# A four-layer convolution chain on one core: tiles kept as sums and differences of neighbours along the width

## The chip, the cores and the metric

The kernel runs on one core of a Trainium2 chip. A core has TensorE (matrix products, PE in the profile, with its weight loads as PEld), VectorE (DVE), ScalarE (ACT), GpSimd (POOL) and SyncE (SP, which here issues most of the DMA transfers). Data lies in the chip's memory (HBM) and is brought into the on-chip buffer (SBUF) by DMA; TensorE writes its products to PSUM, from where VectorE and ScalarE take them. The metric is the device time of one execution, in microseconds (us). Before the change it is 2877.34 us, the median of three runs (2877.28 to 2879.65).

## What is computed

The input x has 4 images of 64 channels of 256 x 256 fp32 values. Four layers follow one another.

Layers 0, 1 and 3 are long convolutions. For each channel c the filter is an outer product of one vector along the rows and one along the width, so that the convolution is two one-dimensional ones, each cut to the first 256 outputs, and a residual:

```
k = jnp.einsum('ijk,imk->ijmk', hx, hy)[0]
...
y = jnp.fft.irfft2(u_f * k_f, s=(fft_size, fft_size))[..., :L, :L]
out = y + x * bias[:, None, None]
```

The vectors hx and hy come from a small network of sines. Layer 2 is a Haar transform in both directions, two 64 x 64 channel mixes with a soft threshold on every coefficient, the sum of both, the inverse transform and a residual:

```
f1 = haar2d(x)
for i in range(v.shape[0]):
    f4 = jnp.einsum('bchw,oc->bohw', f1 * v[i], conv_w[i])
    acc = acc + jnp.sign(f4) * jax.nn.relu(jnp.abs(f4) - tau[i])
return haar2d(acc, inverse=True) + x
```

The first level of the Haar transform along the width replaces each pair of neighbours by their sum and their difference.

## The kernel before, in words

Each one-dimensional convolution is a product with a 256 x 256 triangular Toeplitz matrix, of which two blocks of 128 x 256 and 128 x 128 are multiplied. `toeplitz` fetches, by one DMA of 256 KB per layer and channel, a tile of 128 x 2 x 256 in which each partition holds the filter vector one place further on (one half for the rows, one for the width). `contract` issues four matmuls: the image tile is the stationary operand, the Toeplitz tile, read backwards, is the moving one. TensorE handles fp32 in two records for each matmul. A channel takes two `contract`s per layer: `first` (rows, then ScalarE copies the product out of PSUM, line 267) and `second` (width, then VectorE adds the residual, line 284). The tile comes out transposed after each, so that two give the image the right way round.

For each of the four images the stages are:

- `convolutions`: 64 channels through layers 0 and 1. Then `pairs` (lines 329 and 330) forms sums and differences of neighbours with two VectorE operations; these go to HBM (`keep`) and into `levels`, the further Haar levels along the width (two levels on VectorE, the shorter ones on GpSimd, lines 342 and 343). `split`, `rest` and `down` do the transform along the rows on TensorE; the coefficients go to HBM.
- `mixing`: 64 groups of coefficients. TensorE mixes channels (line 441), VectorE and ScalarE scale (460, 465), threshold (469 to 480) and add (486) into the large tile `z`. `N_ACT` says how many sixteenths of the scaling ScalarE takes.
- `inverse`: for each channel the inverse transform. `rows` (533, 534) and, for the first 16 channels, `cols` on TensorE; `join` adds the kept sums and differences (line 555) and unfolds them into neighbours (lines 558 and 559); then layer 3 follows (`last`) and the result leaves by a DMA on ScalarE's queue. For the first three images every third channel is put off: its tile goes to HBM (`late`), and `convolution` takes it through layer 3 during the mixing of the last image, leaving on SP's queue.

All stages are put on one time axis in units of a tick. `PLACE` gives each step its offset in ticks, `events` is sorted by that time, and the steps are issued in that order; the tile framework then puts the instructions of each engine into a queue of its own, worked off strictly in order, with waits between engines. The convolutions of image b + 1 are spread over the mixing of image b and end where its inverse begins. `BUFS` and the pools set how many copies of a tile there are.

The filters are made at the start by `filters`; its `end` writes both vectors of a layer to HBM (`pads`), from where `toeplitz` reads.

Of the kernel before, what the change touches and what calls it, by code (L numbers as in the profile page):

```python
# [9 lines left out]
F32 = mybir.dt.float32  # L10
# [6 lines left out]
B, C, S, EMB, ORD = 4, 64, 256, 33, 64  # L17
P = 128
ROW = S + P

GT = 4
BUFS = {"res": 1, "y": 5, "co": 3}

N_ACT = (12, 12, 12, 8)

PLACE = {
    "load": 0.714,
    "a0": 1.643,
# [6 lines left out]
    "y1 sum": 4.429,  # L35
    "pairs": 4.639,
    "keep": 4.929,
# [26 lines left out]
    "y3 sum": 3.542,  # L64
    "out": 4.537,
    "level": 0.6,
# [4 lines left out]
    "l y3 sum": 2.783,  # L71
    "l out": 4.4,
    "l mix load": -0.977,
# [25 lines left out]
def conv_seq_kernel(ctx, tc, x, fz, fw, bias, decay, haar, haar_row, factors, vt, taut, wmix, out):  # L99
# [44 lines left out]
    scales = dram.tile([S // 4 // GT, P, 2, GT, 16], F32, name="scales")  # L144
    pads = [dram.tile([C, 2, ROW], F32, name=f"pad{layer}") for layer in range(3)]
    late = dram.tile([B, C, P, 2, S], F32, name="late")

# [11 lines left out]
    def filters(layer, queue):  # L159
# [32 lines left out]
        def end():  # L192
            ps = bank(f"fo{layer}").rearrange("p m s -> p (m s)")[:, :S]
            nc.tensor.matmul(ps, fw_sb[:, 2 * P : 3 * P], st["h"], start=True, stop=True)
            f = part(ROW)
            nc.vector.memset(f[:, S:], 0.0)
            nc.vector.scalar_tensor_tensor(f[:, :S], ps, dsb[:, S:], dsb[:, :S], ALU.mult, ALU.mult)
            for axis, queue in enumerate((nc.scalar, nc.sync)):
                queue.dma_start(pads[layer][:, axis, :], f[axis * C : (axis + 1) * C])
            st["f"] = f  # L200
# [40 lines left out]
    def toeplitz(layer, c, name):  # L241

        t = tp.tile([P, 2, S], F32, name=name, tag="toep")
        nc.sync.dma_start(t, ap(pads[layer], c * 2 * ROW, [[1, P], [ROW, 2], [1, S]]))
        return t
# [3 lines left out]

    def contract(ps, src, t):  # L250

        for m in range(2):
            nc.tensor.matmul(ps[:, m, :], src[:, 0, m * P : (m + 1) * P], t[:, ::-1], start=True, stop=False)  # L253
            nc.tensor.matmul(ps[:, m, P:], src[:, 1, m * P : (m + 1) * P], t[:, : P - 1 : -1], start=False, stop=True)  # L254

    def first(b, st, key, layer, new):


        def product(c):
            s = st[c]  # L260
            s["p" + new] = bank(f"p{new}_{b}_{c}")
            contract(s["p" + new], s[key], s[layer][:, 0, :])

        def copy(c):
            s = st[c]
            a = s[new] = io.tile([P, 2, S], F32, name=f"{new}_{b}_{c}", tag="mid")
            nc.scalar.copy(a, s["p" + new])  # L267

        return [product, copy]

    def second(b, st, key, layer, res, new, tag, ahead=None):


        def product(c):
            s = st[c]
            if ahead is not None:
                s[ahead] = toeplitz(ahead, c, f"t{ahead}_{b}_{c}")
            s["p" + new] = bank(f"p{new}_{b}_{c}")
            contract(s["p" + new], s[key], s[layer][:, 1, :])

        def residual(c):
            s = st[c]
            y = io.tile([P, 2, S], F32, name=f"{new}_{b}_{c}", tag=tag, bufs=BUFS[tag])
            nc.vector.scalar_tensor_tensor(y, s[res], bsb[:, layer, c : c + 1], s["p" + new], ALU.mult, ALU.add)  # L284
            s[new] = y

        return [product, residual]
# [26 lines left out]
    def convolutions(b, ticks, in_parts=(), border=None):  # L314
# [7 lines left out]
        def load(c):  # L322
            xt = io.tile([P, 2, S], F32, name=f"x_{b}_{c}", tag="in", bufs=3)
            nc.sync.dma_start(xt, x[b, c].rearrange("(k p) w -> p k w", p=P))
            st[c] = {"x": xt, 0: toeplitz(0, c, f"t0_{b}_{c}")}

        def pairs(c):
            v = st.pop(c)["y1"].rearrange("p k (w e) -> p k w e", e=2)
            nc.vector.tensor_add(sums[:, c % 4], v[:, :, :, 0], v[:, :, :, 1])
            nc.vector.tensor_sub(sd[:, c % 8, 1], v[:, :, :, 0], v[:, :, :, 1])  # L330

# [50 lines left out]
        def away(c):  # L382
# [5 lines left out]
        work = zip(  # L388
            ("load", "a0", "a0 copy", "y0", "y0 sum", "a1", "a1 copy", "y1", "y1 sum", "pairs", "keep"),
            [  # L390
                load,
                *first(b, st, "x", 0, "a0"),
                *second(b, st, "a0", 0, "x", "y0", "y", ahead=1),
                *first(b, st, "y0", 1, "a1"),
                *second(b, st, "a1", 1, "y0", "y1", "res"),
                pairs,
                store,
# [111 lines left out]
    def inverse(b, start, put_off):  # L509
# [42 lines left out]
        def join(c):  # L552
            ps = st[c]["pw"]
            t = io.tile([P, 2, 2, P], F32, name=f"t_{b}_{c}", tag="res", bufs=BUFS["res"])
            nc.vector.scalar_tensor_tensor(t, st[c]["r"], 0.5, ps, ALU.mult, ALU.add)
            u = io.tile([P, 2, S], F32, name=f"u_{b}_{c}", tag="y", bufs=BUFS["y"])
            v = u.rearrange("p m (w e) -> p m w e", e=2)
            nc.vector.tensor_add(v[:, :, :, 0], t[:, 0], t[:, 1])
            nc.vector.tensor_sub(v[:, :, :, 1], t[:, 0], t[:, 1])
            st[c]["u"] = u  # L560
# [20 lines left out]
        for c in range(C):  # L581
            for name, stage in zip(("sooner", "early", "fetch", "rows"), (sooner, early, fetch, rows)):
                at(start + c + PLACE[name], stage, c)
            turn = start + c
            if c < 16:
                at(start + c + PLACE["halves"], halves, c)
                at(start + c + PLACE["cols"], cols, c)
                turn += 1
            at(turn + PLACE["join"], join, c)
            if c in put_off:  # L590
                at(turn + PLACE["aside"], aside, c)
            else:
                shift = (0.0, 0.0)
                if put_off:
                    shift = ((-0.27, -0.342), (0.23, 0.158))[c % 3]
                for name, stage in zip(("a3", "a3 copy", "y3", "y3 sum", "out"), last(b, st)):
                    at(turn + PLACE[name] + shift[name[0] != "a"], stage, c)

    def last(b, st, queue=nc.scalar):
        return [  # L600
            *first(b, st, "u", 2, "a3"),
            *second(b, st, "a3", 2, "u", "y3", "co"),
            lambda c: queue.dma_start(out[b, c].rearrange("(k p) w -> p k w", p=P), st.pop(c)["y3"]),
        ]

    def convolution(which, ticks):

        for (b, c), tick in zip(which, ticks):
            st = {}

            def load(c, b=b, st=st):
                u = io.tile([P, 2, S], F32, name=f"v_{b}_{c}", tag="in", bufs=3)
                nc.sync.dma_start(u, late[b, c])
                st[c] = {"u": u, 2: toeplitz(2, c, f"t2_{b}_{c}")}

            for name, stage in zip(("l load", "l a3", "l a3 copy", "l y3", "l y3 sum", "l out"), [load, *last(b, st, nc.sync)]):
                at(tick + PLACE[name], stage, c)
# [156 lines left out]
```

## Time and profile before

| what | value |
|---|---|
| median of three runs | 2877.34 us |
| the profiled execution, its own time | 2875.0 us |
| its span (first to last instruction) | 2873.2 us |
| TensorE busy | 2819.8 us (98%) |
| VectorE busy | 2498.0 us (87%) |
| ScalarE busy | 2080.4 us (72%) |
| GpSimd busy | 339.4 us (12%) |
| DMA, mean | 226 GB/s |

Busy time is the time in which an engine has an instruction in hand; matmuls are pipelined, one begins before the last has ended, and their ends are modelled, so a short gap between two can stay unseen. In the views below, "L284" is line 284 of the kernel, `y<-x,bsb,py` says which tile is written from which, then shapes and counts; "busy, mean" are total us and mean ns of one; the idle time ahead of the group and what ended it follow.

The stages on the span's axis: the start to about 30 us; convolutions of the first image to about 430 us; mixing of the first image together with the second's convolutions to about 900; its inverse to about 1080; the same for the second image (1080 to 1728) and the third (1728 to 2376); mixing of the last image with the channels put off to about 2660; the last inverse to the end.

### The profile page before, as it was taken

How to read it: one execution, taken by the hardware profiler on the slowest of the kernel's cores; microseconds unless marked ns; L12 is line 12 of the kernel's file. 1: busy time of each engine (PE TensorE's matmuls, PEld its weight loads, DVE VectorE, ACT ScalarE, POOL GpSimd, SP SyncE). 2: the span in 40 equal slices, each digit the busy share in tenths (PEclk: the TensorE clock that was granted, in tenths of full speed). 3: DMA queues.
4: the chain of work that ended last, by engine and by line, in shares of the span. 5: the costliest groups of instructions: out<-in, count | busy, mean ns of one | idle time of the engine just before them, and what ended most of it. 6: DMA issues, size and time to landing. Idle time of an engine off the chain costs nothing. (4 is left out here: it accounts for less than half of the span.)

```text
span 2873.2 us, 52387 instructions
## 1 busy us (share of the span) xinstructions
PE 2819.8 (98%) x16566; PEld 2550.2 (89%) x16566; DVE 2498.0 (87%) x4263; ACT 2080.4 (72%) x4950; POOL 339.4 (12%) x644
## 2 busy tenths in 40 slices
PE   8999999999999999999999999999999999999999
PEld 6899998888888898998898998998888998888998
DVE  4655558999999779999999779999999779999985
ACT  2333338999995558998995658999995659998554
POOL 0111111121121001221221001221121000000000
PEclk9999999999999999999999999999999999999999
DMA  5877777666676986777777986777777988787786
GB/s 162 260 231 231 230 234 223 208 211 205 202 213 214 291 251 197 215 213 214 209 207 235 299 257 195 216 213 213 212 208 233 299 265 235 230 238 213 224 241 200
DMA packets 599367, 649.77 MB, mean 226 GB/s; under 512 B 48465, under 2 KB 517044, under 8 KB 598964
## 3 DMA queue, kind: packets, MB, share of 16 engines
q1 hardware_dynamic: 536996, 578.61, 68.2%
q10 hardware_dynamic: 62096, 67.82, 6.7%
q8 instruction: 134, 2.20, 0.3%
q14 instruction: 141, 1.16, 0.1%
HBM read 426.77 MB, written 219.48 MB: 225 GB/s over the span
## 5 line engine op out<-in xcount | busy, mean ns | idle before, releaser
L253 PE MATMUL py<-t,a 128*128 128x256 f32 x3072 | 922.2, 382 | 9.9 <-ACT a L267 9.2
L267 ACT COPY a<-pa 128x512 f32<-128x512 f32 x768 | 478.9, 624 | 495.5 <-PE pa L254 453.4
L465 ACT ACTIVATE f<-px,vt 128x64 f32<-128x64 f32 x2816 | 610.6, 367 | 101.4 <-DVE f L460 101.0
L254 PEld LDWEIGHTS py<-t,a 128*128 128x128 f32 x3072 | 583.4, 190 | 79.3
L254 PE MATMUL py<-t,a 128*128 128x128 f32 x3072 | 590.0, 274 | 0.0
L253 PEld LDWEIGHTS py<-t,a 128*128 128x128 f32 x3072 | 497.3, 191 | 51.1 <-ACT a L267 19.3
L441 PE MATMUL px<-wb,f 128*128 128x256 f32 x2048 | 487.6, 380 | 7.4 <-ACT f L465 7.3
L441 PEld LDWEIGHTS px<-wb,f 128*128 128x128 f32 x2048 | 369.0, 190 | 49.8 <-ACT f L465 10.2
L343 POOL TENSOR_TENSOR sd<-less 128x128 f32<-128x128 f32 (+4 forms) x320 | 192.7, 602 | 1855.5 <-DVE less L342 1537.6
L526 ACT COPY zc<-z 128x512 f32<-128x512 f32 x256 | 281.9, 1104 | 108.4 <-PE pw L534 99.6
L476 DVE TENSOR_TENSOR mag<-mag,vt 128x1024 f32<-128x1024 f32 x256 | 316.6, 1237 | 12.2 <-ACT mag L469 11.3
L480 DVE SCALAR_TENSOR_TENSOR mag<-mag,f 128x1024 f32<-128x1024 f32 x256 | 316.5, 1238 | 0.0
L253 PE MATMUL pa<-t,y 128*128 128x256 f32 x1024 | 308.9, 383 | 6.7 <-DVE y L284 5.2
L253 PE MATMUL pa<-t,x 128*128 128x256 f32 x1024 | 305.7, 380 | 0.0
L469 ACT ACTIVATE mag<-f 128x1024 f32<-128x1024 f32 x256 | 295.7, 1155 | 2.7 <-DVE z L486 0.4
L366 DVE TENSOR_TENSOR sp<-sd,sp 128x512 fp32r<-128x512 f32 x256 | 179.8, 702 | 127.8 <-ACT sp L361 126.7
L472 ACT ACTIVATE f<-f 128x1024 f32<-128x1024 f32 x256 | 285.8, 1116 | 3.5
L253 PE MATMUL pa<-t,u 128*128 128x256 f32 x772 | 232.1, 382 | 6.5 <-ACT w L540 2.8
L284 DVE SCALAR_TENSOR_TENSOR y<-x,bsb,py 128x512 f32<-128x512 f32 x256 | 190.7, 745 | 42.1 <-PE py L254 41.8
L254 PEld LDWEIGHTS pa<-t,y 128*128 128x128 f32 x1024 | 194.5, 190 | 26.3
L254 PEld LDWEIGHTS pa<-t,x 128*128 128x128 f32 x1024 | 194.6, 190 | 26.3
L284 DVE SCALAR_TENSOR_TENSOR y<-y,bsb,py 128x512 f32<-128x512 f32 x256 | 190.6, 745 | 27.7 <-PE py L254 27.3
(72 smaller groups left out, 4406.6 us busy)
## 6 DMA issues: line engine op xcount, KB each, us to landing
t<-pad SPq DMA_DIRECT2D x768, 256.0 KB, 4.1
x<-in_x SPq DMA_DIRECT2D x256, 256.0 KB, 3.8
coef<-co SPq DMA_DIRECT2D x256, 256.0 KB, 3.2
f<-coef SPq DMA_DIRECT2D x256, 256.0 KB, 3.1
r<-keep SPq DMA_DIRECT2D x256, 256.0 KB, 4.1
out_y<-y ACTq DMA_DIRECT2D x193, 256.0 KB, 4.2
keep<-sums SPq DMA_DIRECT2D x256, 128.0 KB, 2.9
keep<-sd SPq DMA_DIRECT2D x256, 128.0 KB, 2.8
```

The costliest lines, as they stand in the source:

```text
L253: nc.tensor.matmul(ps[:, m, :], src[:, 0, m * P : (m + 1) * P], t[:, ::-1], start=True, stop=False)
L254: nc.tensor.matmul(ps[:, m, P:], src[:, 1, m * P : (m + 1) * P], t[:, : P - 1 : -1], start=False, stop=True)
L267: nc.scalar.copy(a, s["p" + new])
L284: nc.vector.scalar_tensor_tensor(y, s[res], bsb[:, layer, c : c + 1], s["p" + new], ALU.mult, ALU.add)
L343: engine.tensor_tensor(t[:, :, :, half:length], v[..., 0], v[..., 1], ALU.subtract)
L441: nc.tensor.matmul(ps[:, q, h, :], f[:, q, h * P : (h + 1) * P], wb.rearrange("p r n -> p (r n)"), start=True, stop=True,)
L465: nc.scalar.mul(f4[:, j], px[:, j], scale(g, 0)[:, j : j + 1])
L469: nc.scalar.activation(mag, st[g]["f4"], AF.Abs)
L472: nc.scalar.activation(st[g]["f4"], st[g]["f4"], AF.Sign)
L476: nc.vector.tensor_sub(mag, mag, over(g, 1, 16))
L480: nc.vector.scalar_tensor_tensor(mag, mag, 0.0, st[g]["f4"], ALU.max, ALU.mult)
L526: nc.scalar.copy(a.rearrange("p h k i -> p (h k) i"), z[:, c // 16, :, :, c % 16].rearrange("p i x -> p x i"))
```

## The change

Every image tile of layers 0, 1 and 3 is now kept as sums and differences of neighbours along the width, as `[128, 4, 2, 64]`: for each row half and width half, 64 sums and then 64 differences. The rows' convolution does not mind. For the width, the Toeplitz matrix is written in this basis: a block that takes sums (or differences) gives outputs as sums and as differences, and the two outputs lie side by side in memory. TensorE therefore reads the moving operand with a step of two elements, and the product arrives in PSUM as 64 sums, 64 differences and so on, contiguous.

- The host lays x out in rows of the two halves, with even and odd places apart, and puts the output together again; x and the output move as 2 KB per partition.
- `pairs` is now ahead of layer 0: two adds on GpSimd form sums and differences of x (`butterflies`). The two operations of `pairs` behind layer 1 are gone; the residual of layer 1 (line 284 before) is now two operations of 256 values, which write `sums` and `sd` directly.
- `join` loses its unfolding (558, 559) and its single operation of 512 (555) becomes two of 256 that write the tile `u`.
- Behind layer 3 comes a new step `neighbours`: two adds on GpSimd (on VectorE for the very last channel) unfold the result into `out`, which the DMA then takes.
- The filters: the rows' vector goes to `pads` as before, the width's is turned by six VectorE operations on 64 partitions into pairs (`runs`) and written to HBM. `toeplitz` issues two DMAs instead of one, of 128 KB each.
- Tiles x, xb, y0, u, v and out share the buffers `y`, now 9; `res` is gone. x is loaded 1.7 ticks earlier; "out" leaves 0.66 ticks later ("l out" 0.4).

```diff
-    "load": 0.714,
+    "load": -1.0,
+    "pairs": 0.1,
+    "bands": 0.714,
...
-    "pairs": 4.639,
...
-    "out": 4.537,
+    "neighbours": 3.543,
+    "out": 5.2,
...
-    "l out": 4.4,
+    "l neighbours": 3.48,
+    "l out": 4.8,
...
-            for axis, queue in enumerate((nc.scalar, nc.sync)):
-                queue.dma_start(pads[layer][:, axis, :], f[axis * C : (axis + 1) * C])
+            nc.sync.dma_start(pads[layer], f[:C])
+            g0, g1, g2 = (f[C:, i : i + S : 2] for i in range(3))
...
+            nc.vector.tensor_add(sums, g0, g2)
+            nc.vector.tensor_sub(less, g0, g2)
+            nc.vector.scalar_tensor_tensor(w[:, 0, :P, 0], sums, 0.5, g1, ALU.mult, ALU.add)
+            nc.vector.tensor_scalar(w[:, 0, :P, 1], less, -0.5, None, ALU.mult)
+            nc.vector.tensor_scalar(w[:, 1, :P, 0], less, 0.5, None, ALU.mult)
+            nc.vector.scalar_tensor_tensor(w[:, 1, :P, 1], sums, -0.5, g1, ALU.mult, ALU.add)
+            nc.scalar.dma_start(runs[layer], w)
...
-        nc.sync.dma_start(t, ap(pads[layer], c * 2 * ROW, [[1, P], [ROW, 2], [1, S]]))
+        nc.sync.dma_start(t[:, 0], ap(pads[layer], c * ROW, [[1, P], [1, S]]))
+        nc.sync.dma_start(
+            t[:, 1],
+            ap(runs[layer], c * 4 * RUN, [[2 * RUN, 2], [2, H], [1, S]]),
+        )
...
+    def along_width(ps, src, t):
+
+        t = t.rearrange("p (h n e) -> p h e n", e=2, h=2)[:, ::-1, :, ::-1]
+        v = ps.rearrange("p k (h e n) -> p k h e n", h=2, e=2)
+        for k in range(2):
+            for m in range(2):
+                nc.tensor.matmul(
+                    v[:, k, 1] if m else v[:, k],
+                    src[:, m, k * P : (k + 1) * P],
+                    t[:, 0] if m else t,
...
+    def butterflies(engine, t, name):
+
+        new = io.tile([P, 4, 2, H], F32, name=name, tag="y", bufs=BUFS["y"])
+        engine.tensor_add(new[:, :, 0], t[:, :, 0], t[:, :, 1])
+        engine.tensor_sub(new[:, :, 1], t[:, :, 0], t[:, :, 1])
+        return new
...
+            if new == "y1":
+                for e, to in enumerate((sums[:, c % 4], sd[:, c % 8, 1])):
+                    to = to.rearrange("p k (h n) -> p (k h) n", h=2)
+                    nc.vector.scalar_tensor_tensor(to, s[res][:, :, e], scale, ps[:, :, e], ALU.mult, ALU.add)
...
         def pairs(c):
-            v = st.pop(c)["y1"].rearrange("p k (w e) -> p k w e", e=2)
-            nc.vector.tensor_add(sums[:, c % 4], v[:, :, :, 0], v[:, :, :, 1])
-            nc.vector.tensor_sub(sd[:, c % 8, 1], v[:, :, :, 0], v[:, :, :, 1])
+            st[c]["x"] = butterflies(nc.gpsimd, st[c]["x"], f"xb_{b}_{c}")
...
-            nc.vector.scalar_tensor_tensor(t, st[c]["r"], 0.5, ps, ALU.mult, ALU.add)
-            u = io.tile([P, 2, S], F32, name=f"u_{b}_{c}", tag="y", bufs=BUFS["y"])
-            v = u.rearrange("p m (w e) -> p m w e", e=2)
-            nc.vector.tensor_add(v[:, :, :, 0], t[:, 0], t[:, 1])
-            nc.vector.tensor_sub(v[:, :, :, 1], t[:, 0], t[:, 1])
+            u = io.tile([P, 4, 2, H], F32, name=f"u_{b}_{c}", tag="y", bufs=BUFS["y"])
+            r, w = (t.rearrange("p e k (h n) -> p e (k h) n", h=2) for t in (st[c]["r"], ps))
+            for e in range(2):
+                nc.vector.scalar_tensor_tensor(u[:, :, e], r[:, e], 0.5, w[:, e], ALU.mult, ALU.add)
...
+        def neighbours(c):
+            engine = nc.vector if b + 1 == B and c + 1 == C else nc.gpsimd
+            st[c]["y3"] = butterflies(engine, st[c]["y3"], f"out_{b}_{c}")
```

## The prediction

> **What bounds the kernel now.** I read the page's busy line first, then a table of busy time by stage, then the groups of instructions by shape, then the timeline of GpSimd and VectorE in the mixing stage.
>
> ```profile
> PE 2819.8 (98%) x16566; PEld 2550.2 (89%) x16566; DVE 2498.0 (87%) x4263; ACT 2080.4 (72%) x4950; POOL 339.4 (12%) x644
> ```
>
> TensorE is busy in all but 53.4 of 2873.2 us, at a granted clock of 1.00. An edit that only relieves another engine can win from these pauses alone. By stage (window, its length, then PE, PEld, DVE, ACT, POOL busy):
>
> ```profile
> 432.00:936.00 504.00, 492.23 (x2771) 438.92 (x2770) 488.31 (x818) 435.31 (x1177) 90.49 (x150) 1.00 0.70 210
> 936.00:1080.00 144.00, 141.24 (x930) 130.58 (x930) 107.39 (x212) 83.10 (x121) 0.00 (x0) 1.00 0.87 272
> 1080.00:1512.00 432.00, 429.83 (x2413) 386.99 (x2412) 425.80 (x700) 386.28 (x1085) 89.88 (x140) 1.00 0.71 210
> ...
> 2376.00:2664.00 288.00, 278.39 (x1523) 248.32 (x1522) 285.32 (x413) 268.73 (x686) 0.00 (x0) 1.00 0.77 228
> ```
>
> The reader should see two things. In the mixing stages VectorE is as full as TensorE (488 of 504, 426 of 432). In the last one (2376 to 2664) VectorE, at 285 of 288, is the fuller, and there the change takes nothing from it. The groups that the change touches or that price it:
>
> ```profile
> L253 PE MATMUL py<-t,a 128*128 128x256 f32 x3072 | 922.2, 382 | 9.9 <-ACT a L267 9.2
> L254 PE MATMUL py<-t,a 128*128 128x128 f32 x3072 | 590.0, 274 | 0.0
> L526 ACT COPY zc<-z 128x512 f32<-128x512 f32 x256 | 281.9, 1104 | 108.4 <-PE pw L534 99.6 <-DVE z L486 1.8 <-PE pu L547 1.5
> L284 DVE SCALAR_TENSOR_TENSOR y<-y,bsb,py 128x512 f32<-128x512 f32 x256 | 190.6, 745 | 27.7 <-PE py L254 27.3
> L361 ACT CAST sp<-sd 128x512 fp32r<-128x512 f32 x256 | 180.2, 704 | 8.1 <-POOL sd L343 8.1
> L555 DVE SCALAR_TENSOR_TENSOR t<-r,pw 128x512 f32<-128x512 f32 x192 | 131.7, 686 | 67.5 <-PE pw L534 58.8 <-DMA r<-keep 5.0
> L329 DVE TENSOR_TENSOR sums<-y 128x256 f32<-128x256 f32 x256 | 108.8, 425 | 2.7
> L558 DVE TENSOR_TENSOR u<-t 128x256 f32<-128x256 f32 x256 | 108.8, 425 | 6.3
> L187 DVE SCALAR_TENSOR_TENSOR z<-z 128x256 f32<-128x256 f32 x27 | 11.2, 423 | 0.4
> L197 DVE SCALAR_TENSOR_TENSOR z<-fo,z 128x256 f32<-128x256 f32 x3 | 1.5, 484 | 3.1 <-PE fo L194 3.1
> ```
>
> Last, GpSimd, which gets the new adds. In the convolutions of the first image (72 to 432) a group of its adds, then the timeline in the mixing stage, GpSimd and VectorE:
>
> ```profile
> L342 POOL TENSOR_TENSOR less<-less 128x128 f32<-128x128 f32 x16 | 6.3, 393 | 0.0
> ```
>
> ```profile
> 714.23 3.86 POOL L343 TENSOR_TENSOR sd<-less 128x128 f32<-128x128 f32 x1 [27.66 <-DVE less L342]
> ```
>
> ```profile
> 714.34 1.22 DVE L476 TENSOR_TENSOR mag<-mag,vt 128x1024 f32<-128x1024 f32 x1
> 715.47 2.36 DVE L480 SCALAR_TENSOR_TENSOR mag<-mag,f 128x1024 f32<-128x1024 f32 x2
> 717.74 0.42 DVE L460 TENSOR_TENSOR f<-px,vt 128x256 f32<-128x256 f32 x1
> ```
>
> An add of 128 values takes 0.39 us in one place and 3.86 us in the other, where it stands until VectorE leaves operations with two SBUF operands (476, 480) for one that reads PSUM (460). I take it that GpSimd advances only while VectorE reads PSUM or is idle.
>
> **The change, part by part.** The sum is against the profiled execution, 2875.0 us (span 2873.2 and 1.8 around it); the median of the runs is 2.3 us above that, and the same 2.3 is added at the end. Under 0.2% (5.8 us) is about what a measurement cannot tell from no change.
>
> *TensorE.* Number and size of the matmuls stay, and the order of its queue all but stays. New is the step of two in the moving operand of `py`: 3072 x 256 + 3072 x 128 = 1.18 million columns. No matmul of the trace reads with a step. From below: VectorE reads with a step of two in line 329 (425 ns) and without one in line 187 (423): 0 us; a gain is excluded, since no matmul gets smaller. From above: ScalarE's copy 526 reads 16 elements apart, 1104 ns against 704 for the cast 361, 0.78 ns per element, times 1.18 million: +921 us. I take 0, since 329 has this very step.
> [...]
>
> *VectorE.* Removed: `pairs`, 256 x (425 + 424 ns) = 217 us; the unfolding in `join`, as many operations of the same 425, 217 us. Halved operations: the residual of layer 1, one of 745 becomes two of 484 (line 197 reads PSUM and a scalar in SBUF like these), +57 us; `join`, one of 685 becomes two. For these 512 to 256 values costs 685 - 256 x 1.02 = 424 (the slope from 423 at 256 in line 187 to 685 at 512), so +0.16 x 256 = +42 us. Sum: 2498 - 217 - 217 + 57 + 42 = 2163 us. In the mixing stages a channel loses 0.85 - 0.22 = 0.63 us; a channel takes 288/38 = 7.6 us there (38 residuals per layer between 1224 and 1512), so VectorE falls from 99% to some 91% and TensorE alone is the bound.
>
> What that is worth: TensorE's pauses between 432 and 2376 are 12 + 3 + 2 in the rows above, 2 in 1512 to 1728 and some 5 in the third image, 24 us. A matmul's record runs on 0.16 us past the start of the next (382 ns recorded, 216 apart in the timeline), so each of some sixty pauses hides that much more: 34 us. VectorE ends some of them directly (residual, `w`, `u`) and others by way of ScalarE, which waited 101 us for line 460. I take 60%: -20 us. Bounds: 0, if ScalarE or instruction supply is next in line everywhere, and -34.
>
> *GpSimd.* 1022 adds of 256 values. Price of one with the port free: 393 ns for 128 and 312 for 64 in the same stretch give 1.27 ns a value, so 556; twice 393 is the upper end, 786. I take 600. In mixing, a channel brings 1.2 us, and a quarter of a `levels` burst (ten adds, 0.2 to 0.4 us each where the port is free, 2.7 in all), 0.7: 1.9 us of free port per 7.6. Free is: two residuals' worth of PSUM reads, 0.75 + 0.97, line 460 with 0.42, and 0.6 idle, together some 2.5 us. It fits (75%). The wait added is that of `a0` for `xb`, and GpSimd runs 1.54 ticks ahead (a tick is 288/41 = 7.0 us, so 10.8 us): a burst of `levels` stretched to 2.7/0.33 = 8 us before a pair is about absorbed. I take 0; lower end 0, since nothing can end sooner by it; the upper end is a rival below. In the inverse stages VectorE mostly reads PSUM, so two thirds of a pair in a 3.0 us tick is free.
>
> The last mixing stage: 63 pairs, 76 us of GpSimd beside a full VectorE. The timeline has line 366 at 0.76 us with GpSimd beside it and 0.69 without, so up to 0.07 us on each operation of two SBUF operands. Four in each of 64 groups, half of them touched: +9; part of it lies in pauses, so I take +6. Ends: 0, and +76 if all of GpSimd's time came out of VectorE's. "l out" on SP now waits for GpSimd, and loads of `f`, `v` and Toeplitz tiles queue behind it; 1.32 ticks (4.2 us each) are left for about 4 us.
> [...]
>
> *DMAs.* SP issues 768 more, 0.36 us each in the timeline: 276 us on a queue that issues about 0.9 ms in all. Between loads it waits for buffers anyway: 0. Bytes stay; x and the output go in 2 KB rows, which can only help the 0.87 share of the inverse: 0.
>
> *Ends.* Six operations on 128 values per filter, 0.29 us each: layer 1's filter starts 0.4 us later and the first product with `runs` finds its tile about on time: +0.5 (0 to +3). The last channel adds two operations of 425 before its DMA: +0.8. Buffers `y`: x, xb and y0 take three of nine per channel, so xb waits for the xb three channels back, freed 0.5 tick earlier: 0.
>
> Sum: 2875.0 - 20 + 6 + 1.3 = 2862.3, plus 2.3: **2865 us**. Its own range, with pauses from 0 to -34 and the last mixing from 0 to +15: 2844 to 2872 and a little over.
>
> **Rivals.**
> *GpSimd comes too late* (slower, 0.25). For: the 3.86 us add, and 75% of the port in use. Against: when TensorE waits, VectorE idles and the port comes free. It decides once VectorE leaves less than 1.9/7.6 = 25% of its time; then each of the 192 channels in mixing waits. At 0.3 us each, +58, less 10 us of the gain that remains: 2877 + 48 = 2925; at 0.1 us, 2887.
> *The step costs TensorE time* (slower, 0.10). `py` takes 3072 x (216 + 110 ns) = 1001 us; each 5% of that is +50 us: 2915 and up, to 3786 at the upper end.
> *VectorE's relief is hidden* (0.17): ScalarE and the last mixing stage hold the same pauses, -5 + 6 + 1: 2875 to 2880.
> *All pauses go* (0.05): -34 and most of 10 in the last mixing: 2835 to 2842.
>
> **How the numbers follow.** Forecast 0.43, the rivals as given. Faster by over 0.2% is below 2871.6: 0.40 of the forecast and 0.05: 0.45. Same: 0.17 hidden and 0.02: 0.19. Slower: 0.36 with 0.01 of the forecast. The range, 2842 to 2925, leaves out the last case, the step and a little of the late GpSimd.
>
> **What would show it.** Right: lines 289 and 275 with the same means (382 and 274 ns); VectorE near 2160 us; TensorE's pauses between 432 and 2376 at half; GpSimd near 1.3 to 2 ms busy. Wrong: 289 with a longer mean than 275 (the step), or waits of PE for POOL `xb`, and of SPq for POOL `out` (GpSimd late).

## The result, and the profile after

The changed kernel takes 3578.03 us (median of four runs, 3576.39 to 3580.83) against 2877.31 us: a ratio of 1.2432, interval 1.2417 to 1.2447, so 24% slower or some 700 us. The forecast was 2865 us with a range up to 2925; it was wrong in sign and size. The profiled execution after has a span of 3576.0 us.

The page of the changed kernel, its busy line, then the busy tenths of TensorE and the DMA engines in 40 slices:

```profile
PE 3069.0 (86%) x16566; PEld 2637.8 (74%) x16566; DVE 2345.1 (66%) x3774; ACT 2083.7 (58%) x4950; POOL 1161.9 (32%) x1666
...
PE   6777777999988889988987879989888788999987
...
DMA  4555555565565665666655665565655666666665
```

TensorE was busy in all but 53 us before; now it stands for 507. No compute engine is full over the span, and the DMA engines, busy for 4 to 6 tenths of the time on the mean, move 182 GB/s where they moved 226. So work seems to wait for transfers although the DMA engines as a whole have room. The chain that ended last could be followed back over some 21% of the span; by line, in shares of the whole span, it has one transfer at its head:

```profile
DMA t<-run 5%; POOL out L301 2%; POOL out L300 2%; PE py L289 1%; DMA r<-keep 1%; PE pa L275 1%; DMA out_y<-out 0%; DMA v<-late 0%; PE px L499 0%; DVE mag L534 0%; DVE mag L538 0%; DVE y L340 0%; PE pw L591 0%; DVE z L544 0%; ACT zc L584 0%
```

Pieces of that chain near the end (start, duration, what):

```profile
3405.43 9.39 DMA t<-run
3414.84 8.79 DMA t<-run
3423.64 8.83 DMA t<-run
3432.49 8.61 DMA t<-run
3441.12 8.73 DMA t<-run
```

From 3395 to 3555 us, in the second half of the last inverse, the chain is nothing but 18 loads of the new width half, one behind the other, 7.4 to 10.0 us each and most of them 8.6 to 9.4. Each is 128 KB, and its time runs from issue to landing, so a wait behind a load still in the air is in it. Before, one load of the whole tile, 256 KB, landed in a median of 4.1 us:

```profile
t<-pad SPq DMA_DIRECT2D x768, 256.0 KB, 4.1
```

The timeline of SP's queue in the first convolutions, after (start, duration, line, what):

```profile
229.83 0.51 SPq L261 DMA_DIRECT2D t<-run  x1
230.43 2.22 SPq L390 DMA_DIRECT2D keep<-sums  x1
232.75 0.38 SPq L391 DMA_DIRECT2D keep<-sd  x1
233.22 0.41 SPq L260 DMA_DIRECT2D t<-pad  x1
```

and the same lines in the kernel before:

```profile
218.54 0.33 SPq L333 DMA_DIRECT2D keep<-sums  x1
218.97 0.39 SPq L334 DMA_DIRECT2D keep<-sd  x1
219.45 0.40 SPq L244 DMA_DIRECT2D t<-pad  x1
```

The transfer's own issue is short (0.51 us), but the next one behind it takes 2.22 us instead of 0.33. So the queue from which nearly all loads come stands as well. Waits of TensorE and ScalarE after that hardly existed before (engine, line, what was waited for, us, times, longest):

```profile
PE pa L275 <- DMA t<-pad: 147.2, 155, 4.9
...
ACT a L315 <- DMA t<-run: 66.6, 16, 10.9
...
PE pa L275 <- POOL xb L301: 59.2, 36, 3.9
```

The third line is the forecast's rival, GpSimd too late. It is the smallest of the three, but not the only sign of it: SP waits 100.4 us for `out` (line 665), and `out` has 4% of the span in the chain above.

By stage, from the first and last mixing product of each image (us; convolutions of the first image and the start, then the mixings and inverses of the images):

| kernel | start and conv. | mix 1 | inv. 1 | mix 2 | inv. 2 | mix 3 | inv. 3 | mix 4 | inv. 4 |
|---|---|---|---|---|---|---|---|---|---|
| before | 447 | 399 | 217 | 435 | 213 | 435 | 210 | 271 | 246 |
| after | 637 | 448 | 285 | 500 | 295 | 499 | 293 | 312 | 308 |
| outermost 2 alone, on the kernel before | 641 | 448 | 283 | 504 | 292 | 503 | 288 | 303 | 308 |
| after, run in two halves | 474 | 420 | 227 | 462 | 231 | 462 | 229 | 313 | 255 |
| the same without the butterflies | 470 | 399 | 212 | 441 | 220 | 440 | 215 | 274 | 250 |
| and with a step of one | 469 | 396 | 212 | 435 | 218 | 435 | 213 | 272 | 243 |

Two shapes of loss are in it. After, all stages are longer, most of all those without mixing. With the run in two halves, 117 of some 200 us lie in the mixings, 56 in the inverses and 27 at the start.

### The profile page after: what moved, and what is told of

It is laid out like the page before. It is cut to its first block, busy times and chain, and to the rows that moved or that the text cites. A ratio compares the mean times of both kernels' runs of the same rounds, so it can differ in the third digit from the quotient of the medians.

```text
span 3576.0 us, 54536 instructions
## 1 busy us (share of the span) xinstructions
PE 3069.0 (86%) x16566; PEld 2637.8 (74%) x16566; DVE 2345.1 (66%) x3774; ACT 2083.7 (58%) x4950; POOL 1161.9 (32%) x1666
## 2 busy tenths in 40 slices
DMA packets 535380, 650.20 MB, mean 182 GB/s; under 512 B 50001, under 2 KB 387316, under 8 KB 534964
## 5 line engine op out<-in xcount | busy, mean ns | idle before, releaser
L289 PE MATMUL py<-t,a 128*128 128x256 f32 (+1 forms) x6144 | 1237.9, 345 | 95.4 <-ACT a L315 91.6
L300 POOL TENSOR_TENSOR xb<-x 128x256 f32<-128x256 f32 x256 | 238.2, 930 | 1487.3 <-DMA x<-in_x 1290.5
L300 POOL TENSOR_TENSOR out<-y 128x256 f32<-128x256 f32 x255 | 215.9, 847 | 903.2 <-DVE y L340 855.2
L275 PE MATMUL pa<-t,y 128*128 128x256 f32 (+1 forms) x2048 | 395.8, 337 | 117.9 <-DMA t<-pad 64.7
L275 PE MATMUL pa<-t,xb 128*128 128x256 f32 (+1 forms) x2048 | 392.9, 335 | 116.1 <-POOL xb L301 59.2
L275 PEld LDWEIGHTS pa<-t,xb 128*128 128x128 f32 x2048 | 335.3, 193 | 167.8 <-issue 68.0
L340 DVE SCALAR_TENSOR_TENSOR y<-u,bsb,py 128x512 f32<-128x512 f32 x193 | 144.0, 746 | 373.2 <-issue 335.0
L340 DVE SCALAR_TENSOR_TENSOR y<-xb,bsb,py 128x512 f32<-128x512 f32 x256 | 190.2, 743 | 229.8 <-issue 107.1
L275 PE MATMUL pa<-t,u 128*128 128x256 f32 (+1 forms) x1544 | 300.0, 339 | 39.6 <-DMA t<-pad 27.6
L275 PEld LDWEIGHTS pa<-t,u 128*128 128x128 f32 x1544 | 260.9, 198 | 73.8 <-PE pw L592 33.5
```

The lines of the kernel that those rows point to most:

```text
L275: nc.tensor.matmul(ps[:, m, k * P :], src[:, k, m], t[:, : k * P - 1 if k else None : -1], start=(k == 0), stop=(k == 1),)
L289: nc.tensor.matmul(v[:, k, 1] if m else v[:, k], src[:, m, k * P : (k + 1) * P], t[:, 0] if m else t, start=(m == 0), stop=(m == 1),)
L300: engine.tensor_add(new[:, :, 0], t[:, :, 0], t[:, :, 1])
L340: nc.vector.scalar_tensor_tensor(y, s[res], scale, ps, ALU.mult, ALU.add)
```

## Theories

What differs in the slow transfer is the form of its source: `[[2 * RUN, 2], [2, H], [1, S]]`, two groups of 64 rows. Theory A: the size of the outermost dimension, 2, sets on how many DMA engines the transfer is put. I had not weighed it in the forecast. No view names the engines of a transfer, but the end of the changed kernel speaks for it: SP's last issues are two loads of the width half at 3551.65 and 3552.95 us with one plain load between them, and some 4 us later, when at most these and the rest of two outputs are in the air, the row is (window, length, PE, PEld, DVE, ACT, POOL busy, clock, DMA share of 16 engines, GB/s):

```profile
3557.30:3562.10 4.80, 4.80 (x19) 4.25 (x18) 1.50 (x3) 0.06 (x1) 1.42 (x2) 0.50 0.13 48
```

A share of 0.13 is the time of 2.1 of the 16 engines. The kernel before has 0.54 and 164 GB/s in 2850 to 2854 us, around its last plain loads (issued from 2848.94 us on). For other sizes of the outermost dimension the runs below show the time alone. The rivals: 768 more issues on SP; the pattern's form as such; GpSimd's adds; the step of two. The experiments take them one by one, first on the kernel before, then by undoing parts of the change.

## The experiments

### The pattern alone, and two plain loads, on the kernel before

The kernel before, with the width half fetched by a load of its own from two copies of the vector, the second 64 places on:

```diff
-        nc.sync.dma_start(t, ap(pads[layer], c * 2 * ROW, [[1, P], [ROW, 2], [1, S]]))
+        nc.sync.dma_start(t[:, 0], ap(pads[layer], c * 3 * ROW, [[1, P], [1, S]]))
+        nc.sync.dma_start(t[:, 1], ap(pads[layer], (c * 3 + 1) * ROW, [[ROW, 2], [1, P // 2], [1, S]]))
```

> The kernel before, with one thing added: the width half of each Toeplitz tile is fetched by a DMA of its own whose source has an outermost dimension of two (2 x 64 rows of 1 KB, the second 64 from a shifted copy of the vector), as the changed kernel fetches its pairs. TensorE, VectorE and GpSimd work as before. Theory (the pattern of two confines the transfer to few DMA engines, SP's next issues wait behind it): most of the 700 us, 3200 to 3600. Rival (one more DMA per tile on SP is what costs): as dear as the run with two plain DMAs. Rivals (the step of two costs TensorE, or GpSimd is late): 2870 to 2900, since neither is in this kernel.

Measured: 3569.77 us, 1.2402 (1.2377 to 1.2427). Nothing of the new basis is in this kernel, and it is nearly as slow as the changed one; its stages agree with those after within 10 us each. Pieces of the chain of this kernel near the end (start, duration, what):

```profile
3408.18 8.82 DMA t<-pad
3417.02 8.84 DMA t<-pad
3425.87 8.82 DMA t<-pad
```

The other kernel has two loads as well, each of 128 plain rows:

```diff
-        nc.sync.dma_start(t, ap(pads[layer], c * 2 * ROW, [[1, P], [ROW, 2], [1, S]]))
+        for k in range(2):
+            nc.sync.dma_start(t[:, k], ap(pads[layer], (c * 2 + k) * ROW, [[1, P], [1, S]]))
```

> The kernel before, with each Toeplitz tile fetched by two DMAs of 128 rows instead of one, both with a single step over the 128 partitions: 768 more issues on SP, as in the changed kernel, and nothing else. Theory (confinement): 2877, within 15. Rival (number of issues): 3300 or more.

Measured: 2882.99 us, 1.0017 (1.0007 to 1.0026). The 768 extra issues cost some 4 us. They are not the cause.

### The run in two loads of 64 partitions

The changed kernel, with the outermost dimension of 2 taken out of the pattern and into a loop:

```diff
-        nc.sync.dma_start(
-            t[:, 1],
-            ap(runs[layer], c * 4 * RUN, [[2 * RUN, 2], [2, H], [1, S]]),
-        )
+        for i in range(2):
+            nc.sync.dma_start(t[i * H : (i + 1) * H, 1], ap(runs[layer], (c * 2 + i) * 2 * RUN, [[2, H], [1, S]]))
```

> The changed kernel, with the pattern of two undone: the pairs are fetched by two DMAs of 64 partitions each, 1536 more issues on SP than before. Theory (confinement): nearly all of the 700 us goes; what is left is the step of two on TensorE (first records of 231 and 116 ns against 216 and 110 make 3072 x 21 ns = 65 us) and the forecast of -12: 2930, from 2890 to 2980. Rival (number of issues): above 3578. Rival (GpSimd late): above 3300.

Measured: 3072.84 us, 1.0675 (1.0659 to 1.0691): 505 us are back with the same bytes to the same places. Its transfers (KB each, median us from issue to landing):

```profile
t<-run SPq DMA_DIRECT2D x1536, 64.0 KB, 3.4
```

195 us over the kernel before stay, where the theory expected 2890 to 2980 us in all. They must belong to the rest of the change.

### Outermost 4 and 16

Two loads of 64 changed both the size of the outermost dimension and the pattern's form. So the kernel before once more, with 4 (and then 16) copies of the vector, 32 (8) places apart:

```diff
-    pads = [dram.tile([C, 2, ROW], F32, name=f"pad{layer}") for layer in range(3)]
+    pads = [dram.tile([C, 5, ROW], F32, name=f"pad{layer}") for layer in range(3)]
...
+            for j in range(1, 4):
+                nc.scalar.dma_start(pads[layer][:, j + 1, : ROW - j * (P // 4)], f[C:, j * (P // 4) :])
...
-        nc.sync.dma_start(t, ap(pads[layer], c * 2 * ROW, [[1, P], [ROW, 2], [1, S]]))
+        nc.sync.dma_start(t[:, 0], ap(pads[layer], c * 5 * ROW, [[1, P], [1, S]]))
+        nc.sync.dma_start(t[:, 1], ap(pads[layer], (c * 5 + 1) * ROW, [[ROW, 4], [1, P // 4], [1, S]]))
```

> The kernel before with the width half of the Toeplitz tile fetched by a DMA of its own whose source pattern has an outermost dimension of 4 (four copies of the vector in memory, each 32 places further on, and 32 rows from each); the same data arrives. With an outermost 2 this kernel took 3570 us and the last loads stood 8.8 us apart in the chain; with no outer dimension 2883. Theory A, the outermost dimension sets on how many DMA engines the transfer is put: half the duration, about 4.4 us a load; a channel of the last stage takes about 4 us without the change, so the time falls back to 2885 to 3150. Theory B, any pattern of several rows that isn't one plain run of 128 is slow, whatever its outermost size: 3570 again.

> The same with an outermost dimension of 16 (sixteen copies, each 8 places further on, 8 rows from each). Theory A, by the number of engines: all of the loss is gone, 2878 to 2900, with 45 more writes at the start that may cost a few us. Theory B, by the form of the pattern: 3570 again.

Measured: 2910.28 us with 4, 1.0109 (1.0092 to 1.0126), and 2914.26 with 16, 1.0122 (1.0107 to 1.0137). The form of the pattern is the same as with 2; 660 and 656 of its 692 us are gone. The version with 16 missed its expected range by 14 us: most of what it loses lies at the start, where its 45 extra writes of the vector stand, for the first mixing product comes at 479 us instead of 447, and the stages after it sum to 2434 against 2426. With 4 the start is 13 us longer, and the first three inverses together 22. The loads of the version with 16 (KB each, median us from issue to landing), the same median as in the kernel with two plain loads:

```profile
t<-pad SPq DMA_DIRECT2D x1536, 128.0 KB, 3.8
```

SP's queue tells the same: over the whole run, the issue right behind a load of the width half has a median of 1.75 us in the changed kernel and of 1.96 with the outermost 2 alone, but of 0.37 with 4 and 0.34 with 16. So the size of the outermost dimension sets the loss.

Why 2 loses nearly all and 4 nearly nothing can be estimated from the rows. The chain has a load of 8.8 us at a time. The first convolutions after make 128 such loads between about 72 and 637 us, one per 4.4 us, so about two are in the air at a time. Before, the same 128 took 375 us, 2.9 each, and the 64 of the last inverse 246 us, 3.8 each. A load every 4.4 us can't keep up with either. At half the duration, one every 2.2 us, it keeps up with both. That two are in the air is worked out, not seen in a view, and that 4 halves the duration is the author's assumption: no view shows how long a load took with 4.

### The step of two

The version in halves, with the moving operand read in steps of one (its elements are then in the wrong order):

```diff
-        t = t.rearrange("p (h n e) -> p h e n", e=2, h=2)[:, ::-1, :, ::-1]
+        t = t.rearrange("p (h e n) -> p h e n", e=2, h=2)[:, ::-1, :, ::-1]
```

> As the run with two halves, but TensorE reads the width blocks with a step of one (the same elements in another order, so that the width products have wrong values; all work is done). It prices the step. Theory: 65 us less than with the halves alone, 2850 to 2880, and the width matmuls at the means of the rows' (382 and 274 ns). Rival (the step is free and the longer records are something else, DMA traffic for one): no difference to the halves.

Measured: 3053.65 us, 1.0609 (1.0593 to 1.0625): 19 us less, not the 65 that were expected. The opposite edit on the kernel before, its width blocks read with a step of two:

```diff
+    def contract_two(ps, src, t):
+        t = t.rearrange("p (h n e) -> p h e n", e=2, h=2)[:, ::-1, :, ::-1]
+        v = ps.rearrange("p k (h e n) -> p k h e n", h=2, e=2)
+        for m in range(2):
+            nc.tensor.matmul(v[:, m], src[:, 0, m * P : (m + 1) * P], t, start=True, stop=False)
+            nc.tensor.matmul(v[:, m, 1], src[:, 1, m * P : (m + 1) * P], t[:, 0], start=False, stop=True)
...
-            contract(s["p" + new], s[key], s[layer][:, 1, :])
+            contract_two(s["p" + new], s[key], s[layer][:, 1, :])
```

> The kernel before with the filter blocks along the width read by TensorE with a step of two elements (the elements are then in the wrong order, only the time is of use); nothing else is changed. It prices the step alone in a kernel whose TensorE is at 97%. Theory A, every matmul along the width is longer by what the records of the changed kernel show, 15 ns for a row of 256 and 6 ns for a row of 128, and all of it lies on the path: 65 us, 2930 to 2950. Theory B, as beside the butterflies, a third of it: 2890 to 2900. The forecast's price was nothing: 2877.

Measured: 2914.70 us, 1.0131 (1.0116 to 1.0146), 37 us more: between the two theories. Groups of this kernel's TensorE by shape:

```profile
L260 PE MATMUL py<-t,a 128*128 128x256 f32 x3072 | 964.5, 395 | 5.5 <-ACT a L274 5.0 <-DVE y L291 0.2
L261 PE MATMUL py<-t,a 128*128 128x128 f32 x3072 | 603.5, 277 | 0.0
...
L253 PE MATMUL pa<-t,y 128*128 128x256 f32 x1024 | 305.6, 380 | 3.6 <-DVE y L291 2.5 <-DMA t<-pad 1.0
```

The products along the width take 395 and 277 ns, 382 and 274 before; those along the rows, still with a step of one, stay at 380. Busy time sums to 56 us more (964.5 + 603.5 against 922.2 + 590.0). By the distance of starts, 231 against 216 ns and 116 against 110, it would be 3072 x (15 + 6) = 65 us. TensorE's busy time over the span rises by 49 us, and the kernel is 37 us longer.

### Without the butterflies, on VectorE, and beside the kernel before

Three runs on GpSimd's 1022 adds. First the version in halves without them (`pairs` and `neighbours` are empty):

```diff
-            st[c]["x"] = butterflies(nc.gpsimd, st[c]["x"], f"xb_{b}_{c}")
+            pass
...
-            engine = nc.vector if b + 1 == B and c + 1 == C else nc.gpsimd
-            st[c]["y3"] = butterflies(engine, st[c]["y3"], f"out_{b}_{c}")
+            pass
```

> The two-halves kernel without its adds on GpSimd and the last two on VectorE: x goes into layer 0 as it comes and the result leaves as it is, so that the sums and differences of x and their unfolding are left out. Theory (GpSimd's adds hold back VectorE in the mixing stages, where its operations of 1024 values went from 1237 to 1337 ns, and keep ScalarE's queue waiting in the inverses): of the 194 us that the two-halves kernel is above the kernel before, some 120 go, 2920 to 2970; VectorE's means return to some 1240. Rival (what is left comes from the further 1536 issues on SP and the buffers): 3040 or more.

Measured: 2922.51 us, 1.0154 (1.0139 to 1.0169): the adds cost 150 us. Then the version in halves with the adds on VectorE:

```diff
-            st[c]["x"] = butterflies(nc.gpsimd, st[c]["x"], f"xb_{b}_{c}")
+            st[c]["x"] = butterflies(nc.vector, st[c]["x"], f"xb_{b}_{c}")
...
-            engine = nc.vector if b + 1 == B and c + 1 == C else nc.gpsimd
+            engine = nc.vector
```

> The two-halves kernel with all of those adds on VectorE instead of GpSimd. VectorE gets 1022 x 0.42 us = 430 us more, but keeps its own pace. Theory: VectorE's operations of 1024 values return to some 1240 ns; in mixing it has 0.2 us per channel more than in the kernel before, and full as it is this lengthens the three mixings by 20 us each: 2960 to 3040, below the two-halves kernel. Rival (GpSimd's share of the loss is small): 3100 or more, since VectorE was full with less.

Measured: 2999.07 us, 1.0421 (1.0404 to 1.0439). The same adds cost 77 us on VectorE, half of what they cost on GpSimd, and VectorE's first thresholding operation is back at 1222 ns, as expected. Last the kernel before, with 2048 adds of 128 values on GpSimd beside it, whose result nobody reads:

```diff
+    spare = zpool.tile([P, P], F32, name="spare")
+
+    def beside(t):
+        for k in range(2):
+            for _ in range(2):
+                nc.gpsimd.tensor_add(spare, t[:, k, :P], t[:, k, P:])
...
+            at(tick + 1.7, lambda c: beside(st[c]["x"]), c)
...
+                at(turn + 3.543 + shift[1], lambda c: beside(st[c]["y3"]), c)
...
+            at(tick + 3.48, lambda c, st=st: beside(st[c]["y3"]), c)
```

> The kernel before, with GpSimd's new work beside it: four adds of 128 values per channel on x and four on the result of layer 3, into a tile that nobody reads (2048 adds, 0.39 us each with the port free, about what the changed kernel's 1022 adds of 256 take). Nobody waits for them but the buffers of x and y3. Theory (GpSimd slows VectorE): VectorE's means rise by some 7% in the mixing stages, the last mixing grows by about 40 us and the others by 20 to 40 each: 2950 to 3030. Rival (only the wait for GpSimd's results costs): 2875 to 2890.

Measured: 3048.14 us, 1.0591 (1.0575 to 1.0607), 169 us, 18 above the expected range. These adds keep GpSimd busy for longer than the butterflies do (1657.3 us in all, 1310.1 in the version in halves). No instruction waits for them as an operand, and the waits of VectorE for a buffer that they still read come to 26.7 us in 31 places, so this is hardly a late GpSimd. It is seen on VectorE. Groups of two thresholding operations and the add into `z`, which read SBUF alone, first of the version in halves with the butterflies, then of the one without (count, busy us, mean ns):

```profile
L532 DVE TENSOR_TENSOR mag<-mag,vt 128x1024 f32<-128x1024 f32 x256 | 342.1, 1337 | 20.6 <-ACT mag L525 20.2
L536 DVE SCALAR_TENSOR_TENSOR mag<-mag,f 128x1024 f32<-128x1024 f32 x256 | 339.1, 1325 | 2.6 <-DVE mag L532 0.5
L542 DVE TENSOR_TENSOR z<-mag 128x256 f32<-128x256 f32 x512 | 257.6, 535 | 1.1
```

```profile
L532 DVE TENSOR_TENSOR mag<-mag,vt 128x1024 f32<-128x1024 f32 x256 | 312.1, 1219 | 20.7 <-ACT mag L525 20.0
...
L542 DVE TENSOR_TENSOR z<-mag 128x256 f32<-128x256 f32 x512 | 199.5, 423 | 1.1
```

With the adds about, the first and the third are 118 and 112 ns longer, for an operation of 1024 values as for one of 256 (line 536 took 1225 without them, 100 less). VectorE's busy time over the span is 2356.9 against 2210.0 us: 147 us more, 129 of it in the mixings. The mixings are 103 us longer by the table above, the inverses 45. In the inverses VectorE's busy time grows by 8 us only, so the longer operations don't explain those 45; in the last one ScalarE waits 61.4 us for `out` from GpSimd, a late result as in the rival, but how much of the 45 is lateness was not tested apart. The kernel with the unread adds has the same groups at 1254, 1315 and 521 ns, where the kernel before has 1237, 1238 and 437. In the first mixing (540 to 840 us) the busy row of the version in halves, and of the one without the butterflies (window, length, then PE, PEld, DVE, ACT, POOL):

```profile
540.00:840.00 300.00, 290.69 (x1567) 252.88 (x1566) 297.92 (x437) 272.06 (x774) 142.70 (x161) 1.00 0.71 198
```

```profile
540.00:840.00 300.00, 300.00 (x1647) 266.27 (x1646) 293.73 (x460) 284.77 (x816) 56.09 (x100) 1.00 0.76 209
```

With the adds, VectorE is the full engine there (297.92 of 300) and gets through 437 operations instead of 460; TensorE falls to 290.69.

### Outputs apart

The version in halves, with the two outputs 128 places apart instead of side by side, so that TensorE reads with a step of one and in the right order (`runs` and the reading of the tile are changed to match):

```diff
-            nc.sync.dma_start(t[i * H : (i + 1) * H, 1], ap(runs[layer], (c * 2 + i) * 2 * RUN, [[2, H], [1, S]]))
+            nc.sync.dma_start(
+                t[i * H : (i + 1) * H, 1].rearrange("p (o n) -> p o n", o=2),
+                ap(runs[layer], (c * 2 + i) * 2 * RUN, [[1, H], [RUN, 2], [1, P]]),
+            )
```

> The two-halves kernel with the two outputs of a block kept 128 places apart instead of side by side: TensorE reads with a step of one and all values are right, but the DMAs fetch twice as many rows of 512 bytes. Theory (the step costs 19 us as in the run with the unit step, and DMA engines at 0.7 to 0.85 busy bear the short rows): 3040 to 3070. Rival (short rows cost DMA time that the convolutions of the first image and the inverses have not): 3090 or more.

Measured: 3078.29 us, 1.0687 (1.0671 to 1.0703), no gain over 3072.84, and between the theory and the rival. TensorE's busy time falls by 44 us (2885.0 against 2929.5), but the first convolutions, with twice as many rows to fetch, each of 512 bytes, are 18 us longer. About what the step costs TensorE, the shorter rows seem to cost the loads.

### The relief alone

Two runs without butterflies. The first is the version in halves with a step of one as well; the second takes back the separate loads too, so that of the change little more than VectorE's shorter list is left (and the 2 KB rows of x and the output, and the build of the filters):

```diff
-        nc.sync.dma_start(t[:, 0], ap(pads[layer], c * ROW, [[1, P], [1, S]]))
-        for i in range(2):
-            nc.sync.dma_start(t[i * H : (i + 1) * H, 1], ap(runs[layer], (c * 2 + i) * 2 * RUN, [[2, H], [1, S]]))
+        nc.sync.dma_start(t, ap(pads[layer], c * ROW, [[1, P], [0, 2], [1, S]]))
```

> The version that fetches the run with two DMAs of 64 partitions and has no butterflies on GpSimd, now also read by TensorE with a step of one (the elements are then in the wrong order, and the sums and differences of x and the unfolding of the output are left out, so only the time is of use). Beside the butterflies the step was worth 19 us. Theory A, the step's price per matmul lies on the path once GpSimd is quiet: up to 65 us of longer matmul records (15 ns on each row-of-256 one, 6 ns on each row-of-128 one), so 2860 to 2890. Theory B, it is mostly hidden behind VectorE as it was before: 2895 to 2910. If the time stays at 2922, the step costs nothing here and the 44 us over the kernel before are of the transfers.

> As the run beside it without butterflies and with a step of one, but the Toeplitz tile is fetched as the kernel before fetches it, by one DMA of 256 rows, with the row vector twice (so the products along the width are wrong, and the sums and differences are left out). What is left of the change is VectorE's shorter list: half of the filter's build along the width is gone. The forecast's term, VectorE's relief is worth 20 us (0 to 34): 2845 to 2877. The rival, the relief is hidden behind TensorE: 2875 to 2885. If it is over 2890, something else of the change costs time that has not been named.

Measured: 2894.62 us, 1.0059 (1.0042 to 1.0076), and 2882.53, 1.0015 (1.0005 to 1.0024). The first lies at the edge of its theory B, the second in the range of *the relief is hidden*. So without the adds the step is worth 28 us and the loads 12, and what is left is 5 us slower than the kernel before, not 20 faster. VectorE has 298 us less to do in it (2200.5 busy). The second mixing of the kernel before, then of this one (same columns):

```profile
1063.00:1498.00 435.00, 432.83 (x2428) 389.76 (x2427) 423.14 (x705) 386.42 (x1093) 86.34 (x132) 1.00 0.71 208
```

```profile
1066.00:1501.00 435.00, 432.81 (x2428) 389.47 (x2427) 401.37 (x654) 384.60 (x1093) 87.37 (x136) 1.00 0.83 209
```

VectorE is 22 us emptier and TensorE's pauses are the same 2.2 us: the stage takes 435 us in both. The reduction is real, and in this stage nothing waits for it. Of the 5 us, the start has 6 (the first mixing product at 453 us, not 447). The run's loads read each row twice and are not quite those of before (DMA share 0.83 against 0.71), so that a few us more or less are not settled by it.

## Why the prediction was wrong

The runs make a ladder of medians from the kernel before to the changed one, each rung one part, as far as the parts can be had singly: 2877 to 2883 (VectorE's shorter list, filters and host layout: +5), to 2895 (the run fetched separately, in two loads: +12), to 2923 (step of two: +28), to 3073 (adds on GpSimd: +150), to 3578 (outermost 2 instead of two loads: +505). The order matters: put alone on the kernel before, the outermost 2 costs 692 and hides nearly all of the rest, for the changed kernel lies only 8 us above it.

- *DMAs: "SP issues 768 more ... Between loads it waits for buffers anyway: 0. Bytes stay"*. This is the step that failed: the sum has the transfers at 0, and they cost most of the 700 us. The count of issues was right and costs 4 us, and the bytes did stay (650.20 MB against 649.77). The 2 KB rows helped a little: the queue with most of the output (q10, 68 MB) had the 16 engines for 5.9% of 3074.3 us in the version in halves, 181 us, and before for 6.7% of 2873.2, 193 us. What I didn't price was the form of the new source pattern, which was in the diff. With an outermost 2 a load took some 8.7 us for 128 KB, the issue behind it on SP 2.2 us instead of 0.33, and the pattern cost 505 us in this kernel, 692 alone. No load of the kernel before has so small an outermost dimension in its source, so the price was unknown and needed a bound from above; I gave no bound but 0. By that size, on the kernel before, 2 loses 692 us, 4 and 16 some 31 and 35, of which 13 and 32 lie at the start; how many engines carry a load is shown for 2 alone, by the share of 0.13.
- *GpSimd: lateness 0, and +6 in the last mixing*. The mechanism of the +6, interference with VectorE's operations on two SBUF operands, was right; its size and place were wrong. I priced it with up to 0.07 us on half of the operations, in the last mixing alone, since elsewhere VectorE was to have room. The runs show 100 to 118 ns on the mean over the thresholding operations and the adds into `z`, 103 us over all four mixings, and 150 us in all (169 with unread adds). The adds themselves took 0.85 to 1.14 us each on the mean, in the version in halves, against the 0.6 that I took. What the forecast calls the port is its assumption that GpSimd advances only while VectorE reads PSUM or is idle. It rested on one add of 3.86 us and was not shown: beside the unread adds, three adds of GpSimd (0.39, 0.38 and 0.38 us) end between 565.43 and 566.12 us, while VectorE goes from line 299 through 495 to 373, all on SBUF alone. The rival *GpSimd comes too late* had the sign, but for the mixings another mechanism: the unread adds cost as much without anybody waiting for their result. In the inverses it may have had a part. Moving the adds to GpSimd made them dearer: on VectorE they cost 77 us, on GpSimd 150.
- *TensorE: the step of two is free*. It isn't: 395 ns against 382 for 256 columns, 277 against 274 for 128, +37 us on the kernel before. The lower bound rested on VectorE's row 329, and a row of VectorE's turned out to say nothing of how TensorE reads. It was a rival at 0.10 with 2915 and up; alone on the kernel before it comes to 2914.70. That this meets the rival's 2915 is luck, since the 2915 was the forecast of 2865 and 50 us more, while the step cost 37 us on 2877.
- *VectorE: 2498 to 2163 us, worth -20*. The list is shorter about as said: 2201 to 2210 without the adds. I had not reckoned that neighbouring records overlap by some 0.08 to 0.09 us (in the timeline of the forecast line 476 ends at 715.56 and line 480 begins at 715.47), so that 512 operations fewer save less busy time than their durations. The worth was wrong: TensorE's pauses in the second mixing stay at 2.2 of 435 us. I took 60% of pauses for VectorE's because VectorE was as full as TensorE; being as full is not the same as being waited for. The rival *relief is hidden*, 2875 to 2880, describes what this part does (2882.5).
- *Ends: +1.3*. In the run with the relief alone the start is 6 us longer.
- *Its own range, 2844 to 2872*. The upper end doesn't follow from its terms: with no pause won and +15 in the last mixing they come to 2875.0 + 15 + 1.3 + 2.3 = 2894 us. The stated range reached to 2925 all the same, through the rivals, and the result lies far above both.
- *What would show it*: the forecast's sign of a costly step (289 longer than 275) came, 407 ns against 385 to 398 by tile; so did the waits for `xb` and `out`. The sign for the main cause was not on the list.

The granted clock over the changed execution was 0.973 (0.956 in the kernel with the outermost 2 alone, and 1.00 before), so up to 0.027 x 3069 = 83 us of it could be slower matmuls. It goes with the pattern, since with two loads it is 0.995; why it falls is not settled.

No version ran that beats the kernel before: its relief alone is worth nothing, and each other part of the change costs time here.

## What to carry to other kernels

Read the source pattern of each new DMA for the size of the outermost dimension before counting issues and bytes: a 2 there turned a hidden load into the bound (692 us, put alone on the kernel before), and a pattern with 4 or 16 outside took all but 31 and 35 us of that away, as in the changed kernel a loop over two plain loads gave back 505 us. To relieve an engine is worth the pauses that this engine ends, and that is best asked by a run with the relief alone. Adds given to an idle GpSimd beside a full VectorE came back here as longer VectorE operations (423 to 535 ns for the add into `z`), and cost 150 us where the same adds on VectorE cost 77.

## What the runs showed of the hardware that was not expected

- A load of 128 KB with an outermost 2 took mostly 8.6 to 9.4 us from issue to landing in the last inverse, against a median of 4.1 for 256 KB in one plain load, and the issue that follows it on SP's queue took 1.7 to 2.3 us in the stretch looked at, instead of 0.33 to 0.41. Behind the last two such loads the DMA share is 0.13 (2.1 of 16 engines).
- TensorE's fp32 products with a step of two in the moving operand: 395 against 382 ns, starts 231 against 216 ns apart.
- VectorE's operations on two SBUF operands, of 256 and of 1024 values (lines 542 and 532 of the version in halves), both grew by about 0.11 us on the mean beside GpSimd's adds (423 to 535 ns, 1219 to 1337).
- A transfer with an outermost 4 was already as good for this kernel as one with 16 (2910 and 2914 us).
